# A part of one unit's attention moved beside the last MLP, and TensorE's order of the final two units written out

## The chip, the cores and the metric

The kernel runs on one core of a Trainium2 chip. The core has five engines with a queue each: TensorE (PE in the profile, its weight loads PEld), VectorE (DVE), ScalarE (ACT), GpSimd (POOL) and SyncE (SP), which here only issues DMA. The metric is the device time of one execution in microseconds. Three runs of the kernel before took 1056.87, 1057.65 and 1057.70 us; the median is 1057.65 us.

## The reference

Two transformer blocks are applied to x of shape (32, 64, 512), float32 throughout. Block 0 is attention with one key and value head and a gated MLP of width 2048; block 1 is attention alone, with a latent of width 128 for keys and values. Block 1, which the change is about, is:

```
mu  = mean(x); var = mean(square(x - mu))
h   = (x - mu) * rsqrt(var + eps) * (1 + scale[:, None]) + shift[:, None]
q   = h @ Wq.T                      # 16 heads of 32
c   = h @ Wkd.T                     # the latent, 128 wide
k   = c @ Wku.T ; v = c @ Wvu.T     # 4 heads of 32
q, k rotated by position
out = x + (softmax(q @ k.T / sqrt(32)) @ v) @ Wo.T
```

The sequence length is 64, so the mask of the reference hides nothing.

## The kernel before

**Tiling.** The 32 sequences are cut into eight units of four sequences (256 tokens). A unit lies in SBUF as four chunks of 128 features by 256 tokens. For each unit, `attention0` (block 0's attention and the norm before the MLP), the MLP and `attention1` (all of block 1) follow each other. The MLP is computed with seven products in place of eight for each two by two block (`first_products`, `last_products`, `down`), and the sums of a unit's down products fill four of the eight PSUM banks until its last step adds them to x (lines 969 to 983).

**Staging.** Pieces of different units are interleaved by generators. Each piece issues some matrix products and the work that follows them, then yields an estimated PE cost and a latency. `Order.run` takes the piece whose job has done the smallest share of its total, among those whose latency is over. While the MLP of unit u runs, `attention0` of unit u+1 and, through the job `chain`, `attention1` of units 0 to 5 run beside it (lines 1062 to 1076). `second(u)` yields at no cost until `down` has marked unit u as finished, and then runs `attention1(u)`.

**The tail.** When the MLP of unit 7 is through but for its last down step, that step and `second(6)` and `second(7)` are left (lines 1079 to 1114). They are jobs of rising rank: the down step first, then unit 6, then unit 7. Both units use a "lean" form of `attention1`. Its norm takes the mean as four accumulated products straight from x (eight matmul records, since one float32 product gives two records), squares by halves, sums the squares on PE by quarters (`root_by_quarters`), and spreads the root back over the partitions with four small products (`spread_out`). The form used beside the MLP instead adds the four chunks on POOL first and takes one product for each mean (`total_of`, `mean_of`), and its root is one operation over 256 columns.

**Order on the engines.** The program is handed to a scheduler that decides each engine's order from dependencies and its own estimate of time. Program order guides it but doesn't bind it. Only inside `with ordered(tc, PE)` (line 96) is PE's order that of the program; before the change this is used for the start of the kernel alone (`FIRST`, lines 1045 to 1047).

**Buffers.** Tiles of one tag share a fixed number of slots. In the tail `homes["now"]` lets small products take PSUM banks from all three tags (`at` 2, `gu` 2, `acc` 4) in turn. A dictionary for each of the two units (`sixth`, `seventh`) names the spare SBUF tiles that its values go to.

The steps that the prediction names are: `mean_of` (L466), the differences and squares (L758, L761), the scale on POOL (L763), `root_by_quarters` (L478, L470, L471), `spread_out` (L400), the second scale and shift (L771, L774), the projections (L525, named lat, q and po by their banks), keys and values (L804, L806), `rotate` (L533 to L536), the mask on the keys (L822), the copies of values (L828), the scores (L845), `softmax` (L545 to L555), `turned` (L560, L561), the contexts (L869, L878), and `output` (L573, L576).

Of the kernel before, what the change touches and what calls it, by code (L numbers as in the profile page):

```python
# [13 lines left out]
ALU = mybir.AluOpType  # L14
# [32 lines left out]
WARM = 11  # L47
STAY = 14103
FIRST = "aaaaaaa bb a mm aa bb a bbb aa b mm a bb aa a m b a b m b a b".replace(" ", "")
TWO_PI = float(np.nextafter(np.float32(2 * np.pi), np.float32(0)))  # L50


# [56 lines left out]
def two_blocks(ctx: ExitStack, tc: tile.TileContext, a: dict, out: bass.AP):  # L109
# [38 lines left out]
    make_identity(nc, ident)  # L148
    ones = fixed([P, P])
    nc.gpsimd.memset(ones, 1.0 / D)  # L150

    idle = bank("at", "idle")
    for _ in range(WARM):
        nc.tensor.matmul(idle[:, :P], ones, ones, start=True, stop=True)

    spread = fixed([P, US, P])
    nc.gpsimd.memset(spread, 0.0)
# [329 lines left out]
    def root_row(parts, eps, room, name):  # L487

        r = space(room, "r", UT, f"r_{name}")[:, :S]
        root_by_quarters(parts, eps, r, f"qs_{name}")  # L490
        pr = abank(f"row_{name}")[:, :UT]
        spread_out(pr.rearrange("p (b s) -> p b s", s=S), r)
        return pr
# [67 lines left out]
        nc.scalar.copy(pT, pp.rearrange("p c t -> p (c t)"))  # L561
        return pT

    def output(u, cT, w, name, last=False):

        x = x_units[u]
        for h in range(2):
            po = abank(f"po_{name}_{h}").rearrange("p (c t) -> p c t", c=2)
            for c in range(2):
                o = 2 * h + c  # L570
                project(po[:, c], w, slice(o * P, (o + 1) * P), cT)
            part = slice(2 * h, 2 * h + 2)
# [169 lines left out]
    def attention1(u, room):  # L742
        vb = room.get("vb", vblk1[u % 2])
        x = x_units[u]
        lean = "lean" in room
        h = tile4(room, "h", f"h1_{u}")
        if lean:
            mean = mean_of([x[:, k] for k in range(KC)], f"mean_{u}")
        else:
            sums = work("sq", [P, KC, UT], f"sum_{u}", 1)  # L750
            total = space(room, "tot", UT, f"tot_m{u}")
            nc.gpsimd.tensor_tensor(sums[:, 0:2], x[:, 0:2], x[:, 2:4], ALU.add)
            nc.gpsimd.tensor_tensor(total, sums[:, 0], sums[:, 1], ALU.add)
            yield 0.0, 6.0
            mean = mean_of([total], f"mean_{u}")
        sq = tile4(room, "h", f"sq1_{u}") if lean else work("sq", [P, KC, UT], f"sq1_{u}", 1)
        for part in (slice(0, 2), slice(2, 4)) if lean else (slice(0, 4),):
# [4 lines left out]
        parts = [sq[:, k] for k in range(KC)] if lean else [total_of(room, sq, f"v{u}")]  # L762
        nc.gpsimd.tensor_tensor(by_seq(h), by_seq(h), per_seq(s1, u), ALU.mult)  # L763
        yield 0.43, 3.0 if lean else 9.0
        if lean:
            r = root_row(parts, eps1, room, f"c{u}")
# [3 lines left out]
        for part in (slice(0, 2), slice(2, 4)) if lean else (slice(0, 4),):  # L770
# [3 lines left out]
            nc.gpsimd.tensor_tensor(by_seq(h[:, part]), by_seq(h[:, part]), per_seq(t1, u)[:, part], ALU.add)  # L774
        yield 0.43, 5.5 if lean else 9.0

        lat = abank(f"lat_{u}")
        project(lat[:, :UT], wkd, slice(0, LAT), h)
# [20 lines left out]

        query(0)  # L800
        yield 3.4, 0.0

        kv = abank(f"kv1_{u}")
        nc.tensor.matmul(kv[:, :UT], wkv1[:, 0], latT, start=True, stop=True)  # L804
        for t in range(2):
            nc.tensor.matmul(  # L806
                kv[:, UT + t * P : UT + (t + 1) * P], latT[:, t * P : (t + 1) * P], wkv1[:, 1], start=True, stop=True
            )
        kr = space(room, "kr", UT, f"kr_{u}").rearrange("p (b s) -> p b s", s=S)
        few = [P, US, S]  # L810
        rotate(
            kr,
            kv[:, :UT].rearrange("p (b s) -> p b s", s=S),
            cos.unsqueeze(1).to_broadcast(few),
            sin.unsqueeze(1).to_broadcast(few),
            few,
            f"k1_{u}",
        )
        kb = space(room, "kb", 2 * UT, f"kb1_{u}").rearrange("p (b g s) -> p b g s", b=US, g=2)
        wide = [P, US, 2, S]  # L820
        mask = kmask.unsqueeze(1).unsqueeze(3).to_broadcast(wide)
        nc.gpsimd.tensor_tensor(kb, kr.unsqueeze(2).to_broadcast(wide), mask, ALU.mult)  # L822
        for t in range(2):
            for b in range(2):
                v = kv[b * S : (b + 1) * S, UT + t * P : UT + (t + 1) * P]
                v = v.rearrange("p (m r d) -> p m r d", m=2, r=2)
                for r in range(2):
                    nc.scalar.copy(  # L828
                        vb[r * S : (r + 1) * S, 2 * t + b, :, r * HD1 : (r + 1) * HD1], v[:, :, r, :]
                    )  # L830
        yield 0.9, 0.0

        query(1)
        yield 3.4, 4.5

        cT = tile4(room, "h", f"cT1_{u}")
        def scores(t):
# [21 lines left out]
        def context(t, ps):  # L859
            pTs = []  # L860
            for m in range(2):
                name = f"1_{u}_{t}_{m}"
                pT = turned(ps[m], name, space(room, "pT", 512, f"pT{name}"))
                pTs.append(pT.rearrange("p (j t) -> p j t", j=4))
                yield 0.5, 1.2 * m
            cx = abank(f"cx1_{u}_{t}").rearrange("p (b c s) -> p b c s", b=2, c=KC)
            for b in range(2):
                for m in range(2):
# [10 lines left out]
            yield 1.0, 1.5 * t  # L879

        ps = []
        for t in range(2):
            ps.append(scores(t))

            yield 0.9, (0.0, 6.0)[t] if lean else 9.0
            if not lean:
                yield from context(t, ps[t])
# [170 lines left out]
    def behind():  # L1058
        for u in range(6):
            yield from second(u)  # L1060

    chain = Job(behind(), 0.8 * A1)
    for u in range(NU):
        now = Job(mlp(u), M)
# [15 lines left out]
    def spare(tag, cols, name, bufs=2):  # L1080
        return work(tag, [P, cols], f"own_{name}", bufs)

    zeros = spare("pT1", 512, "vb7", 2).rearrange("p (b r d) -> p b r d", b=US, r=2)
    nc.gpsimd.memset(zeros, 0.0)
    two = [spare("h2", 1024, f"h2{i}") for i in range(2)]
    few = spare("cs", 512, "few", 1)
    extra = spare("x", 1024, "kb6", XB)
    sixth = {
        "ring": "0",
        "lean": True,  # L1090
        "vb": vblk1[0],
        "p": [t[:, j * 512 : (j + 1) * 512] for t in two for j in range(2)],
        "latT": [few[:, :UT]],
        "kr": [few[:, UT:]],
        "kb": [extra[:, :512]],
        "pT": [extra[:, 512:], spare("pT0", 512, "pT6", 2)] * 2,
    }
    big = [spare("mw", 1792, f"mw{j}", MW) for j in range(4)]
    seventh = {
        "ring": "-",  # L1100
        "lean": True,
        "vb": zeros,
# [5 lines left out]
        "pT": [big[1][:, 1024:1536], big[2][:, 1024:1536]] * 2,  # L1108
# [86 lines left out]
```

## Time and profile before

| what | value |
|---|---|
| median of three runs | 1057.65 us |
| profiled execution, its own time | 1055.26 us |
| its span, first to last instruction | 1053.4 us |
| mean granted clock of TensorE | 0.989 |
| PE busy | 1012.6 us (96%) |
| PEld busy | 938.7 us (89%) |
| DVE / ACT / POOL busy | 546.7 / 329.1 / 432.8 us |
| MLP of unit 7, last product of its last down step | ends at about 980.4 us |
| last product of the kernel | ends at about 1049.6 us |

The span is the distance from the first to the last instruction of the profiled execution; its own time is 1.86 us longer, and 2.39 us shorter than the median of the runs. A timeline row is start, length, engine, line, operation and operands; successive rows of PE overlap a little, since matmuls are pipelined, so the work of a group is read from its start to the start of the next. In a table of stretches the columns are the length of the stretch, the busy time of each engine with its instructions, the granted clock (1.00 is full), the DMA share and GB/s.

### The profile page before, as it was taken

To read this page: it belongs to the slowest core of one execution; us is meant where nothing else is said; L and a number is where in the kernel's file an instruction comes from. 1 tells how busy PE (TensorE), PEld (TensorE's weight loads), DVE (VectorE), ACT (ScalarE), POOL (GpSimd) and SP (SyncE) were. 2 spreads that over 40 slices of the span, in tenths; PEclk is the share of its full clock that TensorE was granted. 3 is DMA by queue.
4 is the path that set the end of the run, shared out by engine and by line. 5 is a ranking of instruction groups with operands and counts; after the bars stand their busy time and mean duration, and the time that the engine had idled before them with its cause. 6 is when DMAs were issued, how large, how long until landed. Compare 5 with 4: busy or idle time off the path is not lost.

```text
span 1053.4 us, 21591 instructions
## 1 busy us (share of the span) xinstructions
PE 1012.6 (96%) x8602; PEld 938.7 (89%) x8602; DVE 546.7 (52%) x1377; ACT 329.1 (31%) x680; POOL 432.8 (41%) x518
## 2 busy tenths in 40 slices
PE   7899999999999999999999999999999999999887
PEld 6679999998999889989999989999999899999765
DVE  4966646545355385353555286532655345352363
ACT  4342112255114243142431332341424422141132
POOL 3424545443255443355341544234632335432541
PEclk8989999999999999999999999999999999999899
DMA  8816896463666364663555565465735547564001
GB/s 277 310 61 218 288 303 247 151 211 122 234 210 211 108 244 152 219 243 127 212 178 181 207 209 183 141 214 187 277 117 194 202 165 280 204 229 170 11 1 40
DMA packets 68275, 198.55 MB, mean 188 GB/s; under 512 B 7248, under 2 KB 15184, under 8 KB 67792
## 3 DMA queue, kind: packets, MB, share of 16 engines
q1 hardware_dynamic: 68176, 197.17, 53.4%
q8 instruction: 69, 1.13, 0.4%
q14 instruction: 30, 0.25, 0.1%
HBM read 180.37 MB, written 16.78 MB: 187 GB/s over the span
## 4 chain that ended last, share of the span: by engine, by line
PE 81%; DVE 8%; POOL 5%; DMA 2%; issue 2%; ACT 1%; SPq 0%; ACTq 0%; POOLq 0%; DVEq 0%
PE gu L899 34%; PE down L958 17%; PE po L525 10%; PE q L525 9%; DMA set<-in_wmlp 2%; PE cx L869 2%; PE sc L845 1%; PE lat L525 1%; PE pp L560 1%; PE sc L673 1%; PE kv L525 1%; PE cx L694 1%; DVE sm L553 1%; PE tab L400 1%; DVE mx L545 1%
## 5 line engine op out<-in xcount | busy, mean ns | idle before, releaser
L899 PE MATMUL gu<-h,set 128*128 128x128 f32 x2048 | 288.1, 277 | 6.4 <-DVE c L918 5.7
L899 PEld LDWEIGHTS gu<-h,set 128*128 128x128 f32 x2048 | 258.8, 192 | 15.5 <-issue 10.4
L899 PE MATMUL gu<-hc,set 128*128 128x128 f32 x1536 | 215.2, 275 | 0.0
L899 PEld LDWEIGHTS gu<-hc,set 128*128 128x128 f32 x1536 | 193.5, 192 | 1.0 <-issue 0.6
L937 POOL TENSOR_TENSOR act<-c,c 128x384 f32<-128x384 f32 x64 | 66.4, 1038 | 210.5 <-DVE c L925 140.8
L958 PE MATMUL down<-td,set 128*128 128x128 f32 x1024 | 137.5, 276 | 3.3 <-POOL td L940 2.5
L958 PEld LDWEIGHTS down<-td,set 128*128 128x128 f32 x1024 | 125.4, 192 | 5.2 <-POOL td L940 3.5
L911 ACT COPY e<-gu 128x128 f32<-128x128 f32 x128 | 33.7, 264 | 259.9 <-PE gu L899 246.8
L525 PE MATMUL q<-h,stays 128*128 128x256 f32 x480 | 111.3, 385 | 1.5 <-POOL h L774 1.5
L525 PE MATMUL po<-cT,stays 128*128 128x256 f32 x480 | 109.0, 382 | 2.1 <-DVE sm L553 2.1
L958 PE MATMUL down<-act,set 128*128 128x128 f32 x768 | 109.5, 278 | 0.0
L925 DVE TENSOR_TENSOR c<-gu,u 128x256 f32<-128x256 f32 x128 | 53.4, 419 | 106.4 <-PE gu L899 106.1
L525 PEld LDWEIGHTS q<-h,stays 128*128 128x128 f32 x480 | 90.9, 193 | 14.3 <-POOL h L774 1.7
L525 PEld LDWEIGHTS po<-cT,stays 128*128 128x128 f32 x480 | 89.8, 191 | 14.0 <-ACT cT L878 2.6
L958 PEld LDWEIGHTS down<-act,set 128*128 128x128 f32 x768 | 97.6, 192 | 5.2 <-issue 3.2
L913 DVE TENSOR_TENSOR u<-e,gu 128x128 f32<-128x128 f32 x128 | 35.9, 281 | 127.5 <-ACT e L911 126.8
L555 POOL TENSOR_TENSOR p<-p,sm 128x512 f32<-128x512 f32 x40 | 41.6, 1058 | 121.4 <-DVE sm L554 113.7
L536 POOL TENSOR_TENSOR qT<-u_q,v_q 128x512 f32<-128x512 f32 x30 | 38.1, 1269 | 97.2 <-DVE v_q L535 97.1
L573 DVE TENSOR_TENSOR x<-x,po 128x512 f32<-128x512 f32 x32 | 22.0, 687 | 87.7 <-PE po L525 87.7
L994 ACT ACT_TABLE_LOAD x34 | 43.6, 1283 | 54.5 <-DVE c L925 54.0
L939 POOL TENSOR_TENSOR td<-act 128x256 f32<-128x256 f32 x64 | 46.7, 730 | 5.6 <-DVE act L936 0.9
L994 ACT ACTIVATE c<-gu 128x128 f32<-128x128 f32 x64 | 17.7, 277 | 90.2 <-DVE c L925 82.2
(269 smaller groups left out, 1333.0 us busy)
## 6 DMA issues: line engine op xcount, KB each, us to landing
set<-sums SPq DMA_DIRECT2D x168, 512.0 KB, 5.6
set<-in_wmlp SPq DMA_DIRECT2D x192, 384.0 KB, 4.6
sums<-set SPq DMA_DIRECT2D x24, 512.0 KB, 4.1
x<-in_x SPq DMA_DIRECT2D x8, 512.0 KB, 5.5
out_x<-x SPq DMA_DIRECT2D x16, 256.0 KB, 2.3
mod<-in_mod SPq DMA_DIRECT2D x7, 512.0 KB, 5.2
a<-in_wmlp SPq DMA_DIRECT2D x24, 128.0 KB, 3.1
stays<-in_wo SPq DMA_DIRECT2D x2, 1024.0 KB, 8.0
```

The source lines that it names most:

```text
L525: nc.tensor.matmul(ps, w[:, k, cols], h[:, k, :], start=(k == 0), stop=(k == KC - 1))
L536: nc.gpsimd.tensor_tensor(dst, u, v, ALU.add)
L555: nc.gpsimd.tensor_tensor(p8, p8, sm.unsqueeze(2).to_broadcast(wide), ALU.mult)
L573: nc.vector.tensor_tensor(x[:, part], x[:, part], po, ALU.add)
L899: nc.tensor.matmul(ps, w[:, slot, k * P : (k + 1) * P], b[of][:, k], start=start and k == 0, stop=k == 1, skip_group_check=True)
L911: nc.scalar.copy(e, ps[:, 0])
L913: nc.vector.tensor_tensor(u2, e, ps[:, 1], ALU.add)
L925: nc.vector.tensor_tensor(c.rearrange("p (a b) t -> p a b t", b=2)[:, :, 1], ps[:, 2:4], u2.unsqueeze(1).to_broadcast([P, 2, HT]), ALU.add,)
L937: nc.gpsimd.tensor_tensor(act[:, 1:4], gate[:, 1:4], c[:, 1:4], ALU.mult)
L939: nc.gpsimd.tensor_tensor(td[:, 0:2], act[:, 1:3], act[:, 0:2], ALU.subtract)
L958: nc.tensor.matmul(sums_of[u][p][:, c], w[:, slot, c * P : (c + 1) * P], b[of], start=q % NP == 0 and i % 2 == 0 and c == 0, stop=q % NP = ...
L994: nc.scalar.activation(gate[2][:, 0], gate[0][:, 0], AF.Silu)
```

## The change

The change has four parts.

1. **Part of unit 6 moves beside the MLP of unit 7.** `second(6)` is made before the loop over the units, and while the MLP of unit 7 runs, `some` takes its first four pieces with a cost (`EARLY`): two of the norm, one of the latent, one of keys and values. In this part the norm has the form used beside the MLP (`slim` is false where a room is `early`), and keys and values come before the queries.
2. **The order of the tail on PE is written out.** After the loop, the last down step is issued, and then the string `LAST` gives the order of the remaining pieces: a for unit 6, b for unit 7, i for two products whose result nobody reads. The whole is inside `ordered`, so PE keeps it.
3. **Pieces are cut finer and reordered.** A lean query gives up its turn after each of its two chunks, the lean norm between the root and its spreading, and in the lean form all transposes of both halves (`turn`) come before the contexts. `output` in the lean form adds and stores each chunk by itself: four stores of 128 KB in place of two of 256 KB for a unit.
4. **Buffers.** The spare tiles of unit 6 are declared earlier, and both units have four separate places for transposed probabilities, where they had two used twice.

```diff
+EARLY = 4
+LAST = "aa b aa b iii b aa ii b bb bbb aa aa bb aa aaaa bbbb bb bbbb".replace(" ", "")
...
+    def idle(n):
+        idles["n"] += 1
+        ps = abank(f"idle_{idles['n']}")
+        for _ in range(n):
+            nc.tensor.matmul(ps[:, :P], ones, ones, start=True, stop=True)
...
         root_by_quarters(parts, eps, r, f"qs_{name}")
+        yield 0.5, 1.0
         pr = abank(f"row_{name}")[:, :UT]
...
+                if fine:
+                    nc.vector.tensor_tensor(x[:, o], x[:, o], po[:, c], ALU.add)
+                    nc.sync.dma_start(out[u][:, o], x[:, o])
+                    yield 1.7, 0.0
...
+        early = "early" in room
+        slim = lean and not early
...
-        if lean:
+        if slim:
             mean = mean_of([x[:, k] for k in range(KC)], f"mean_{u}")
...
+                if lean and c == 0:
+                    yield 1.7, 0.0
...
+        queries = [query(i) for i in range(2)]
+        if early:
+            kb = keys_values()
+            yield 0.9, 0.0
+        elif lean:
+            yield next(queries[0])
+            kb = keys_values()
+            yield 0.9, 0.0
+        for i, q in enumerate(queries):
+            yield from q
+            yield 1.7 if lean else 3.4, 4.5 * i
...
         if lean:
-            yield from context(0, ps[0])
-            yield from context(1, ps[1])
-        yield from output(u, cT, wo1, f"1_{u}", True)
+            pTs = []
+            for t in range(2):
+                pTs.append((yield from turn(t, ps[t])))
+            for t in range(2):
+                context(t, pTs[t])
+                yield 1.0, 1.5 * t
+        yield from output(u, cT, wo1, f"1_{u}", True, lean)
...
+    sixth = second(6, room6)
+    def some(pieces, n):
+        for cost, latency in pieces:
+            n -= cost > 0
+            yield cost, latency
+            if not n:
+                return
...
+        if u == NU - 1:
+            jobs.append(Job(some(sixth, EARLY), 5.0))
         chain.done -= chain.total if u > 1 else 0.0
         rest = order.run(jobs, until=tuple(must))
+    order.run([*rest, Job(down(NU * NP - 1), 3.0)])
     homes["now"] = everywhere
...
-    last = down(NU * NP - 1)
-    tail = [Job(second(6 + i, room), A1, 2 + i) for i, room in enumerate((sixth, seventh))]
-    order.run([*rest, Job(last, 3.0, 1), *tail])
+    ends = {"a": sixth, "b": second(7, room7)}
+    with ordered(tc, mybir.EngineType.PE):
+        for name in LAST:
+            if name == "i":
+                idle(2)
+            else:
+                next(ends[name])
+        for pieces in ends.values():
+            assert next(pieces, None) is None
```

More of the change, by code (lines that the diff above doesn't have):

```diff
@@ L150, in two_blocks @@
     nc.gpsimd.memset(ones, 1.0 / D)
-    idle = bank("at", "idle")
-    for _ in range(WARM):
-        nc.tensor.matmul(idle[:, :P], ones, ones, start=True, stop=True)
+    idles = {"n": 0}
+    def idle(n):
[3 more added lines that the diff above has]
+            nc.tensor.matmul(ps[:, :P], ones, ones, start=True, stop=True)
+    idle(WARM)
     spread = fixed([P, US, P])
@@ L562, in turned, with output @@
         return pT
-    def output(u, cT, w, name, last=False):
+    def output(u, cT, w, name, last=False, fine=False):
         x = x_units[u]
@@ L571, in output @@
                 project(po[:, c], w, slice(o * P, (o + 1) * P), cT)
+                if fine:
+                    nc.vector.tensor_tensor(x[:, o], x[:, o], po[:, c], ALU.add)
+                    nc.sync.dma_start(out[u][:, o], x[:, o])
+                    yield 1.7, 0.0
+            if fine:
+                continue
             part = slice(2 * h, 2 * h + 2)
@@ L755, in attention1 @@
             mean = mean_of([total], f"mean_{u}")
-        sq = tile4(room, "h", f"sq1_{u}") if lean else work("sq", [P, KC, UT], f"sq1_{u}", 1)
-        for part in (slice(0, 2), slice(2, 4)) if lean else (slice(0, 4),):
+        sq = tile4(room, "h", f"sq1_{u}") if slim else work("sq", [P, KC, UT], f"sq1_{u}", 1)
+        for part in (slice(0, 2), slice(2, 4)) if slim else (slice(0, 4),):
             nc.vector.tensor_tensor(
@@ L761, in attention1 @@
             nc.scalar.activation(sq[:, part], h[:, part], AF.Square)
-        parts = [sq[:, k] for k in range(KC)] if lean else [total_of(room, sq, f"v{u}")]
+        parts = [sq[:, k] for k in range(KC)] if slim else [total_of(room, sq, f"v{u}")]
         nc.gpsimd.tensor_tensor(by_seq(h), by_seq(h), per_seq(s1, u), ALU.mult)
-        yield 0.43, 3.0 if lean else 9.0
-        if lean:
-            r = root_row(parts, eps1, room, f"c{u}")
+        yield 0.43, 3.0 if slim else 9.0
+        if slim:
+            r = yield from root_row(parts, eps1, room, f"c{u}")
         else:
@@ L769, in attention1 @@
             inverse_root(mean_of(parts, f"var_{u}"), eps1, r)
-        for part in (slice(0, 2), slice(2, 4)) if lean else (slice(0, 4),):
+        for part in (slice(0, 2), slice(2, 4)) if slim else (slice(0, 4),):
             nc.vector.tensor_tensor(
@@ L774, in attention1 @@
             nc.gpsimd.tensor_tensor(by_seq(h[:, part]), by_seq(h[:, part]), per_seq(t1, u)[:, part], ALU.add)
-        yield 0.43, 5.5 if lean else 9.0
+        yield 0.43, 5.5 if slim else 9.0
         lat = abank(f"lat_{u}")
@@ L798, in query @@
             )
[L800 to L807, printed above, removed]
-            )
[L809 to L830, printed above, removed]
@@ L831, in attention1, with keys_values @@
-        yield 0.9, 0.0
-        query(1)
-        yield 3.4, 4.5
+        def keys_values():
+            kv = abank(f"kv1_{u}")
+            nc.tensor.matmul(kv[:, :UT], wkv1[:, 0], latT, start=True, stop=True)
+            for t in range(2):
+                nc.tensor.matmul(
+                    kv[:, UT + t * P : UT + (t + 1) * P], latT[:, t * P : (t + 1) * P], wkv1[:, 1], start=True, stop=True
+                )
+            kr = space(room, "kr", UT, f"kr_{u}").rearrange("p (b s) -> p b s", s=S)
+            few = [P, US, S]
+            rotate(
+                kr,
+                kv[:, :UT].rearrange("p (b s) -> p b s", s=S),
+                cos.unsqueeze(1).to_broadcast(few),
+                sin.unsqueeze(1).to_broadcast(few),
+                few,
+                f"k1_{u}",
+            )
+            kb = space(room, "kb", 2 * UT, f"kb1_{u}").rearrange("p (b g s) -> p b g s", b=US, g=2)
+            wide = [P, US, 2, S]
+            mask = kmask.unsqueeze(1).unsqueeze(3).to_broadcast(wide)
+            nc.gpsimd.tensor_tensor(kb, kr.unsqueeze(2).to_broadcast(wide), mask, ALU.mult)
+            for t in range(2):
+                for b in range(2):
+                    v = kv[b * S : (b + 1) * S, UT + t * P : UT + (t + 1) * P]
+                    v = v.rearrange("p (m r d) -> p m r d", m=2, r=2)
+                    for r in range(2):
+                        nc.scalar.copy(
+                            vb[r * S : (r + 1) * S, 2 * t + b, :, r * HD1 : (r + 1) * HD1], v[:, :, r, :]
+                        )
+            return kb
@@ L836, in attention1 @@
+        queries = [query(i) for i in range(2)]
[9 more added lines that the diff above has]
+            yield 1.7 if lean else 3.4, 4.5 * i
+            if not lean and i == 0:
+                kb = keys_values()
+                yield 0.9, 0.0
         cT = tile4(room, "h", f"cT1_{u}")
@@ L857, in scores, with turn @@
             return ps
-        def context(t, ps):
+        def turn(t, ps):
             pTs = []
@@ L865, in context @@
                 yield 0.5, 1.2 * m
+            return pTs
+        def context(t, pTs):
             cx = abank(f"cx1_{u}_{t}").rearrange("p (b c s) -> p b c s", b=2, c=KC)
@@ L878, in context @@
                 nc.scalar.copy(to[:, b], cx[:, b])
-            yield 1.0, 1.5 * t
         ps = []
@@ L886, in attention1 @@
             if not lean:
-                yield from context(t, ps[t])
+                pTs = yield from turn(t, ps[t])
+                context(t, pTs)
+                yield 1.0, 1.5 * t
         if lean:
-            yield from context(0, ps[0])
-            yield from context(1, ps[1])
-        yield from output(u, cT, wo1, f"1_{u}", True)
+            pTs = []
+            for t in range(2):
+                pTs.append((yield from turn(t, ps[t])))
+            for t in range(2):
+                context(t, pTs[t])
+                yield 1.0, 1.5 * t
+        yield from output(u, cT, wo1, f"1_{u}", True, lean)
     finished = set()
@@ L1060, in behind, with spare @@
             yield from second(u)
+    def spare(tag, cols, name, bufs=2):
+        return work(tag, [P, cols], f"own_{name}", bufs)
+    two = [spare("h2", 1024, f"h2{i}") for i in range(2)]
+    few = spare("cs", 512, "few", 1)
+    extra = spare("x", 1024, "kb6", XB)
+    room6 = {
+        "ring": "0",
+        "lean": True,
+        "early": True,
+        "vb": vblk1[0],
+        "p": [t[:, j * 512 : (j + 1) * 512] for t in two for j in range(2)],
+        "latT": [few[:, :UT]],
+        "kr": [few[:, UT:]],
+        "kb": [extra[:, :512]],
+        "pT": [extra[:, 512:]] + [spare("pT0", 512, f"pT6{i}", 2) for i in range(2)] + [spare("pT1", 512, "pT62", 2)],
+    }
+    sixth = second(6, room6)
[5 more added lines that the diff above has]
+                return
     chain = Job(behind(), 0.8 * A1)
@@ L1074, in two_blocks @@
             jobs.append(chain)
+        if u == NU - 1:
+            jobs.append(Job(some(sixth, EARLY), 5.0))
         chain.done -= chain.total if u > 1 else 0.0
         rest = order.run(jobs, until=tuple(must))
+    order.run([*rest, Job(down(NU * NP - 1), 3.0)])
     homes["now"] = everywhere
-    def spare(tag, cols, name, bufs=2):
-        return work(tag, [P, cols], f"own_{name}", bufs)
     zeros = spare("pT1", 512, "vb7", 2).rearrange("p (b r d) -> p b r d", b=US, r=2)
     nc.gpsimd.memset(zeros, 0.0)
[L1085 to L1097, printed above, removed]
     big = [spare("mw", 1792, f"mw{j}", MW) for j in range(4)]
-    seventh = {
+    room7 = {
         "ring": "-",
@@ L1107, in two_blocks @@
         "p": [spare(tag, 512, f"{tag}{i}") for tag in ("gate", "act") for i in range(2)],
-        "pT": [big[1][:, 1024:1536], big[2][:, 1024:1536]] * 2,
+        "pT": [big[1][:, 1024:1536], big[2][:, 1024:1536], big[3][:, 512:1024], big[3][:, 1024:1536]],
         "qT": [big[2][:, :1024]],
```

## The prediction

> **What bounds the kernel now.** I read the stretches first: the MLP of unit 7 against what comes after it.
>
> ```profile
> 864.00:980.40 116.40, 115.20 (x994) 111.19 (x993) 49.04 (x133) 30.46 (x70) 43.81 (x58) 1.00 0.60 211
> 980.40:1053.40 73.00, 58.90 (x446) 46.54 (x444) 34.98 (x73) 21.09 (x50) 27.08 (x26) 0.95 0.04 15
> ```
>
> Beside the MLP, PE is busy 115.20 of 116.40 us while DVE, ACT and POOL are busy 49, 30 and 44: a product added there costs its own length, and vector work is free as long as it is not in front of something PE awaits. In the tail PE stands still for 14 of 73 us, and the clock is not full. Next, the PE timeline of the tail shows where.
>
> ```profile
> 980.37 1.89 PE L466 MATMUL mean<-x,stays 128*128 128x256 f32 x8
> 982.93 1.99 PE L466 MATMUL mean<-x,stays 128*128 128x256 f32 x8 [0.67 <-POOL x L982]
> ...
> 986.91 1.08 PE L400 MATMUL row_c<-r_c,stays 128*128 128x64 f32 x8
> 987.92 0.65 PE L478 MATMUL qs_c<-own_mw,stays 128*32 128x64 f32 x30
> 990.09 2.07 PE L525 MATMUL q<-h,stays 128*128 128x256 f32 x4 [1.53 <-POOL h L774]
> 991.96 1.81 PE L400 MATMUL row_c<-own_mw,stays 128*128 128x64 f32 x8
> 993.56 3.48 PE L525 MATMUL lat<-h,stays 128*128 128x256 f32 x8
> ...
> 1003.79 1.89 PE L525 MATMUL lat<-own_mw,stays 128*128 128x256 f32 x8
> ...
> 1017.87 0.65 PE L560 MATMUL pp<-stays,own_h 128*128 128x128 f32 x4 [2.30 <-POOL own_h L555]
> ...
> 1028.70 7.17 PE L525 MATMUL po<-cT,stays 128*128 128x256 f32 x32 [2.10 <-DVE sm L553]
> ```
>
> The waits in this view sum to 10.0 us (0.67, 1.07, 1.53, 2.30, 0.35, 0.73, 2.10, 0.53, 0.74). The same latent takes 1.89 us at 1003.79 and 3.48 at 993.56: the clock. The stretches of it:
>
> ```profile
> 985.00:990.00 5.00, 2.46 (x72) 1.93 (x66) 3.50 (x6) 2.32 (x5) 4.11 (x4) 0.98 0.01 3
> 990.00:997.00 7.00, 6.91 (x21) 5.90 (x22) 1.28 (x2) 0.00 (x0) 3.09 (x4) 0.53 0.00 0
> 1015.00:1019.50 4.50, 1.85 (x12) 1.05 (x10) 3.97 (x11) 1.85 (x3) 2.42 (x3) 1.00 0.00 0
> ```
>
> After five microseconds of small products and waits in the norms, the clock is halved for about 6.8 us, which costs 3.4. From 980.4 the tail is thus about 55 us of products, 10 of waits, 3.4 of clock and 3.8 from the last product (1049.6) to the end.
>
> **Part 1, the early pieces.** Pitches come from the timeline: a chunk of projection (8 records of 256 columns) 1.73 us (1000.34 to 1003.79 for 16), keys and values 0.88 (999.46 to 1000.34). Added to the MLP stage: two means of 2 records each 0.43 + 0.43, latent 1.73, keys and values 0.88, together **3.5 us** of PE, all on the path. Taken from the tail: mean 1.73, sums of squares 0.65, row 1.01, latent 1.73, keys and values 0.88, together 6.0.
>
> The vector work that moves with them, by unit 5's rows in the same stage: POOL two sums (1.27 + 0.73) twice, scale 1.91, shift 1.91, keys 0.72 + 1.06, that is 9.6 us; DVE 1.22 + 1.75 (the root over 256 columns) + 1.21 + 1.3 for the keys; ACT 1.06, 0.47, 0.37, 1.74 and one or two table loads of 1.28. It goes into queues with half their time free, behind which stand the gate's products (L937 to L941) and so `down`. Cover gone, a 1.91 us POOL operation in front of them would hold PE that long. PE's waits for such things sum to some 12 us between 100 and 980 us, about 0.1 in 8 us. I reserve **0.5 us**; bounds are 0 and 9.6 (all of POOL's work uncovered). No DMA moves: these four pieces issue none. The time is ample: unit 6's x is done at about 889 and unit 5's latent came 33 us after its mean, so unit 6's keys fall near 925, with the MLP ending at 984.
>
> **Part 2, the tail's order.** I lay `LAST` out from the end of the last down step, PE in order. Other pitches: scores 1.90, a pair of transposes 0.88, contexts 1.08 for half a unit, sums of squares 0.65, row 1.01, an unread product 4 records for two at 0.112 (12 MLP records from 958.92 to 960.26). From a query's end to its rotated form is 3.42 us (1009.15 to 1012.57: DVE v, u, shuffle, POOL add).
>
> - q6 first half to 3.46; mean of 7 to 5.19. Its x is whole at 2.5 (982.88 before), so it doesn't wait; if it did, the second half of q6 would be queued behind it. q6 second half to 8.65.
> - Sums of squares of 7 to 9.30: its squares are ready by 7.2, behind q6's rotation on DVE. Three idle pieces (1.34) to 10.64. The root takes 1.3 us after the sums (988.57 to 989.85), so is ready near 10.6. Row to 11.65. Queued behind it are unit 6's scores, which wait until 8.65 + 3.42 = 12.07 anyway. The root and that rotation meet on DVE: **0.55** more, one reciprocal.
> - Scores of 6 to 15.87; two idle pieces (0.89) to 16.76. h of 7 is ready by 14.9 (DVE 1.28 and POOL 2.05, after the row), so these 0.89 cover nothing. Latent 18.49; q7 chunk 20.22; keys 21.10; other three chunks 26.29; four transposes of 6 to 28.05. The softmax of 6 had from 14 on; before, four of them took DVE and POOL about 10 us from the first score.
> - Scores of 7 need q7 rotated: 26.29 + 3.42 = 29.71, a **wait of 1.66** with unit 6's contexts and output queued behind it, which could have run. To 33.51. Contexts of 6 to 35.67, copies on ACT 0.72, output of 6 to 43.31. The softmax of 7 takes 10.2 us from 31.6 and is covered by that output.
> - Transposes of 7 to 45.07, contexts 47.23, copies 0.72, output to 54.87, last add 0.42. From the last add's end to the end was 3.06 (1050.34 to 1053.40). [...] I keep 3.06. With the 0.55, the end is at **58.9**.
>
> The tail goes from 73.0 to 58.9, that is 14.1 less: 3.4 clock, 6.0 - 2.2 products, about 6 of waits, 0.3 of the last add. Less 3.5 and 0.5 in the MLP stage, the sum is **-10.1 us**. The profiled execution took 1055.26 and would take 1045.2; its median stands 2.39 higher, so I forecast **1047.5**.
>
> **Part 3 and 4** cost nothing beyond this. The finer adds are 8 of 0.42 against 4 of 0.69 on DVE, of which only the last shows; SP issues 8 stores (0.33 each) against 4, and no load is behind them. The zeros for unit 7's values stay after the loop, 0.53 on POOL, well ahead of use.
>
> [...] From 26.3 to 29.7 PE runs only transposes and waits. The row of 1015.00 holds such a stretch: 2.30 idle, four transposes, 0.35 idle, four more, and the clock was 1.00 throughout. [...]
>
> **Rivals.**
>
> - **The clock falls once more in the tail**, as just said, or in the norm of 7 in spite of the idle products: 1050.9. [...] against it, the row at 1015 and full-size products on both sides.
> - **The MLP stage pays.** Unit 6's POOL and DVE work gets in front of the gate's: two or three of the 1.9 us operations uncovered give 4 us more, 1051.5, up to 9.6 - 0.5 more. Against it: stages before with a whole attention0 beside the MLP (150 to 250 us, DVE 50.6, POOL 45.0 of 100) had PE never idle.
> - **The order on DVE and POOL in the tail** is the scheduler's. If softmax and rotations are served in a poor order, behind a PE that can't step aside, some 5 us of the gain stay: 1052.5.
> - **Slower: unit 6's norm is late.** The scheduler could leave its early pieces to the end of the MLP stage. Then the first piece of `LAST` waits and everything on PE is behind it. From the first sum to h the durations above sum to about 14 us (2.0, 0.6, 1.2, 1.1, 2.0, 0.6, 1.8, 1.75, 1.2, 1.9), with the clock falling (3.4) it ends near 1065. It decides when h of 6 comes more than 10.1 us after the last down step. Against it: 60 us of slack.
>
> **How the numbers follow.** Forecast 0.62; clock 0.12; MLP stage 0.11 (0.08 faster, 0.02 the same, 0.01 slower); order on DVE 0.07 (0.06 and 0.01 the same); late norm 0.08. A change within 0.2% (2.1 us) is about what a measurement can't tell from none. Faster 0.88, same 0.03, slower 0.09. The forecast's own range is 1044.5 to 1050: without any of the waits and reserves (4.6 us: 0.42, 1.66, 0.72, 0.72, 0.55, 0.5) it would be 1042.9, and each could double. The low end of the whole range is that bound, 1042.9; the high end, 1053.5, takes in the clock, the DVE order and an MLP stage with 6 us of waits, and leaves out the late norm and the worst of the stage.
>
> **What would show it.** The latent and keys of 6 before 950 us; the last down step ending 3.5 to 4 later, near 984; full clock in the tail; a wait of one to two microseconds before unit 7's scores; 59 us from the last down step to the end. It is wrong if PE waits for h of 6, if `down` waits on POOL more than before, or if the clock drops again.

## The result, and the profile after

Four runs of the changed kernel took 1047.24 to 1051.62 us with a median of 1048.55, against 1057.64 before: 9.1 us less, a ratio of 0.9918 with a 95% interval of 0.9898 to 0.9937. The forecast was 1047.5 in a range of 1042.9 to 1053.5. The profiled execution took 1047.82 us, its span is 1046.0; before it was 1053.4, so in the profiles only 7.4 us are gained. Line numbers are those of the changed kernel from here on; in the kernels with a bank for each chunk they are one higher from the output on (L912 for L911).

The stretches of the changed kernel first: the MLP of unit 7, in nearly the same window as before, and the tail.

```profile
864.00:980.00 116.00, 115.94 (x987) 111.56 (x987) 53.83 (x138) 36.21 (x82) 50.31 (x61) 1.00 0.60 210
986.08:1046.00 59.92, 49.76 (x404) 40.71 (x402) 31.42 (x68) 17.43 (x38) 21.46 (x21) 1.00 0.06 18
```

Beside the MLP, DVE, ACT and POOL carry 5 to 6.5 us more each, and PE waits no more for them than before: from the mean product of unit 7's norm (ms_b below) to the end of the last down step its one wait in both profiles is 1.2 us for POOL (td, L940 before and L978 after). The tail is 59.9 us where it was 73.0, with 10 us of PE idle where there were 14, and the clock is full throughout. Then the PE timeline of the tail.

```profile
986.08 3.62 PE L535 MATMUL q<-h,stays 128*128 128x256 f32 x16
989.54 1.89 PE L475 MATMUL mean<-x,stays 128*128 128x256 f32 x8
...
997.43 1.08 PE L409 MATMUL row_c<-own_mw,stays 128*128 128x64 f32 x8 [0.44 <-DVE own_mw L480]
998.44 1.30 PE L875 MATMUL sc<-own_kb,qT 64*64 64x128 f32 x34
1000.05 1.10 PE L875 MATMUL sc<-own_kb,qT 64*64 64x128 f32 x30 [0.31 <-DVE own_mw L789]
1001.08 1.16 PE L161 MATMUL idle<-stays 128*128 128x128 f32 x8
1002.07 1.89 PE L535 MATMUL lat<-own_mw,stays 128*128 128x256 f32 x8
...
1015.19 1.54 PE L875 MATMUL sc<-own_mw,own_mw 64*64 64x128 f32 x48 [1.10 <-POOL own_mw L546]
...
1020.19 1.99 PE L535 MATMUL po<-cT,stays 128*128 128x256 f32 x8 [1.58 <-ACT cT L911]
1023.47 3.72 PE L535 MATMUL po<-cT,stays 128*128 128x256 f32 x16 [1.29 <-DVE x L583]
1027.71 1.99 PE L535 MATMUL po<-cT,stays 128*128 128x256 f32 x8 [0.51 <-DVE x L583]
...
1036.60 3.72 PE L535 MATMUL po<-own_mw,stays 128*128 128x256 f32 x16 [0.51 <-DVE x L583]
1040.84 1.99 PE L535 MATMUL po<-own_mw,stays 128*128 128x256 f32 x8 [0.51 <-DVE x L583]
```

PE starts on unit 6's queries at once, and the norm of unit 7 lies under them. What is new is in the outputs: the 32 records that ran without a break are now in pieces of 8, 16 and 8, and each break ends with an add on DVE (L583). In the list of waits of the changed kernel's tail (us in total, times, longest us) these breaks stand first.

```profile
PE po L535 <- DVE x L583: 2.8, 4, 1.3
PE po L535 <- ACT cT L911: 1.6, 1, 1.6
PE sc L875 <- POOL own_mw L546: 1.1, 1, 1.1
PE po L535 <- ACT own_mw L911: 0.7, 1, 0.7
PE row_c L409 <- DVE own_mw L480: 0.4, 1, 0.4
PE sc L875 <- DVE own_mw L789: 0.3, 1, 0.3
```

To set the kernels side by side I use three marks of each profile: the mean product of unit 7's norm before its MLP (ms_b), the first product after the last down step, and the end of the span.

| kernel | ms_b at | MLP stage | tail | median of its runs |
|---|---|---|---|---|
| before | 859.24 | 121.13 | 73.0 | 1057.64 |
| changed | 861.14 | 124.94 | 59.9 | 1048.55 |

The 7.4 us of the profiles are thus 13.1 in the tail, less 3.8 in the MLP stage, less 1.9 ahead of ms_b, where the change did nothing to the work. Over the profiles of the runs below this first mark lies anywhere from 858.40 to 863.09, and for the changed kernel itself at 861.14 and 862.77 in two profiles, so I take the 1.9 for chance. Without it the two stages give 9.3 us, close to the 9.1 of the medians.

### The profile page after: what moved, and what is told of

It reads as the page before. It is cut to its first block, busy times and chain, and to the rows that moved or that the text cites. A ratio compares the mean times of both kernels' runs of the same rounds, so it can differ in the third digit from the quotient of the medians.

```text
span 1046.0 us, 21558 instructions
## 1 busy us (share of the span) xinstructions
PE 1007.5 (96%) x8578; PEld 936.4 (90%) x8578; DVE 548.7 (52%) x1379; ACT 334.1 (32%) x683; POOL 436.4 (42%) x521
## 4 chain that ended last, share of the span: by engine, by line
PE 81%; DVE 8%; POOL 4%; DMA 4%; issue 2%; ACT 1%; SPq 0%; ACTq 0%; DVEq 0%; POOLq 0%
PE gu L937 33%; PE down L996 16%; PE q L535 10%; PE po L535 10%; DMA set<-in_wmlp 3%; PE sc L875 2%; PE pp L570 1%; PE cx L902 1%; PE lat L535 1%; PE sc L689 1%; PE kv L535 1%; PE cx L710 1%; DVE set L264 1%; DVE sm L563 1%; DMA x<-in_x 1%
## 5 line engine op out<-in xcount | busy, mean ns | idle before, releaser
L589 DVE TENSOR_TENSOR x<-x,po 128x512 f32<-128x512 f32 x28 | 19.2, 687 | 72.9 <-PE po L535 72.9
```

## The experiments

Two theories stood against each other after the result. The first: the sum of the prediction is right as it stands. The second: it came out near by two errors that cancel, since each unit's scores, charged 3.80 us, took 2 to 2.6, and the outputs, charged 6.92 us each, took 9.35 and 8.73.

The experiments were run in three series, each on another chip and each with the kernel before beside them; its medians were 1056.26, 1056.88 and 1055.56 us. Across series a ratio or the length of a tail is therefore a better measure than a median. A tail is that of one profile; for the changed kernel it was 59.9 and 60.0 in two.

**One add for two chunks.** The output of units 6 and 7 gets back its old form.

```diff
-        yield from output(u, cT, wo1, f"1_{u}", True, lean)
+        yield from output(u, cT, wo1, f"1_{u}", True)
-LAST = "aa b aa b iii b aa ii b bb bbb aa aa bb aa aaaa bbbb bb bbbb"
+LAST = "aa b aa b iii b aa ii b bb bbb aa aa bb aa aa bbbb bb bb"
```

> The output of units 6 and 7 goes back to one add and one store for two chunks; all else is as in the changed kernel. Theory, one bank for two chunks: PE waits for the add of a chunk before it writes the next chunk of the same PSUM bank (2.8 us of waits on L583 in four places, and about 0.26 us of pipeline for each), so the two outputs lasted 9.35 and 8.73 us where their products take 6.92 each. Without it they take 6.9 to 7.2 each, some 3.9 us come back, and the coarser last add and store take 0.6: about 3.3 us less than the changed kernel, near 1045.2. Theory of the prediction, the finer adds cost nothing but their last add: 0.3 to 0.6 us slower than the changed kernel, near 1049. From the last down step to the end: 56.6 us by the first, 60.4 by the second (59.9 in the changed kernel's profile).

Measured: 1044.09 us (1043.12 to 1046.19), ratio to before 0.9886 (0.9861 to 0.9910), a tail of 56.6 against 59.9. The finer output, as the changed kernel has it, costs 3.3 us.

**A bank for each chunk.** The finer adds stay, but no two chunks share a PSUM bank.

```diff
-            po = abank(f"po_{name}_{h}").rearrange("p (c t) -> p c t", c=2)
+            po = None if fine else abank(f"po_{name}_{h}").rearrange("p (c t) -> p c t", c=2)
             for c in range(2):
                 o = 2 * h + c
-                project(po[:, c], w, slice(o * P, (o + 1) * P), cT)
+                pc = abank(f"po_{name}_{o}")[:, :UT] if fine else po[:, c]
+                project(pc, w, slice(o * P, (o + 1) * P), cT)
                 if fine:
-                    nc.vector.tensor_tensor(x[:, o], x[:, o], po[:, c], ALU.add)
+                    nc.vector.tensor_tensor(x[:, o], x[:, o], pc, ALU.add)
```

> The finer adds and stores stay, but each chunk of the output has a PSUM bank to itself. Theory, one bank for two chunks: the four waits on L583 go, 3.9 us less than the changed kernel, near 1044.6, and from the last down step to the end about 56.0 us. Rival, the waits are for the add itself or for DVE's queue, whatever the bank: no change, 59.9 us.

Measured: 1043.97 us (1042.42 to 1044.60), ratio 0.9877 (0.9850 to 0.9904), a tail of 56.0, as expected by the first of its theories. PE's timeline of this kernel has both outputs whole again.

```profile
1020.88 7.17 PE L535 MATMUL po<-cT,stays 128*128 128x256 f32 x32 [1.58 <-ACT cT L912]
...
1032.44 7.17 PE L535 MATMUL po<-own_mw,stays 128*128 128x256 f32 x32 [0.74 <-ACT own_mw L912]
```

So it is what two chunks shared and not the add. In the changed kernel PE begins the second chunk of a bank only when the add that reads the first one has ended: the four adds end at 1023.42, 1027.65, 1036.55 and 1040.78, and PE goes on 0.05 to 0.06 us later. The edit gives each chunk a tile of its own as well as a bank, so whether the dependency was drawn for the bank or for the tile isn't shown. The wait is paid four times: three times 0.51 us, and 1.29 where DVE was still in a softmax. Each time some 0.26 us more is lost at the break, which is an estimate: a row of 8 records lasts 1.99 us after a wait, against 1.73 from start to start in an unbroken row.

**No unread products.**

```diff
-LAST = "aa b aa b iii b aa ii b bb bbb aa aa bb aa aaaa bbbb bb bbbb"
+LAST = "aa b aa b b aa b bb bbb aa aa bb aa aaaa bbbb bb bbbb"
```

> All five pieces of unread products are left out; the order is otherwise the same. Theory of the clock: without them PE has the sums of squares, a wait of about 1.8 us and the row in the norm of unit 7, the clock halves for 6.8 us as before the change, and the kernel is 3.4 - 0.9 = 2.5 us slower than the changed one, near 1051. Rival, PE is busy enough on either side: the clock stays at 1.00 in the tail, the first three pieces only covered a wait, and the last two (0.99 us from 1001.08 to 1002.07) were in the way: 0.9 us faster, near 1047.7.

Measured: 1047.50 us (1046.29 to 1050.40), ratio 0.9919 (0.9892 to 0.9947), a tail of 60.0: no difference. Neither theory foresaw it so. The row started 11.35 us after the last down step as in the changed kernel, since PE waited 1.96 us for the root in place of 1.60 of unread products and 0.44 of waiting. Then the clock did fall in this profile, but for some 3.4 us in place of 6.8 (estimated from the 0.58 below; from 998 to 1001 it was 0.50), and what that cost is what the second place of unread products had cost: from the first score of unit 6 to the end of unit 7's latent both kernels take 5.36 us. The wait and the stretches, without unread products:

```profile
996.15 1.08 PE L409 MATMUL row_c<-own_mw,stays 128*128 128x64 f32 x8 [1.96 <-DVE own_mw L480]
```

```profile
994.00:997.00 3.00, 1.04 (x23) 0.91 (x12) 2.00 (x5) 1.60 (x2) 1.49 (x2) 1.00 0.00 0
997.00:1001.00 4.00, 4.00 (x69) 3.51 (x68) 3.53 (x6) 0.33 (x1) 2.05 (x2) 0.58 0.00 0
```

**The early pieces alone.** The tail is handed back to the job list, and with it to the scheduler's own order. The finer pieces stay; the unread products, which stand in `LAST`, go with it.

```diff
-    ends = {"a": sixth, "b": second(7, room7)}
-    with ordered(tc, mybir.EngineType.PE):
-        for name in LAST:
...
+    tail = [Job(pieces, A1, 2 + i) for i, pieces in enumerate((sixth, second(7, room7)))]
+    order.run(tail)
```

> The early pieces of unit 6 and the finer pieces stay, but the tail is handed to the job list by rank as before the change, with the scheduler's own order on PE and no unread products. If moving the early pieces is most of the gain: near 1049 to 1051. If the written order is most of it: within 2 us of the kernel before, 1056 to 1058. My own sum: early pieces take 6.0 of products and unit 6's norm from the tail and give 3.5 to the MLP, but unit 7's norm has then nothing ahead of it in rank except unit 6's queries, and waits of 4 to 6 us stay; near 1051.5.

Measured: 1061.16 us (1059.23 to 1063.92, 9 runs), ratio to before 1.0050 (1.0035 to 1.0065): slower than before, which none of the three expectations held. The MLP stage is 124.95 us, as with the order; the tail is 74.2. Two of its stretches and two lines of its PE timeline:

```profile
1005.00:1012.00 7.00, 5.49 (x16) 4.19 (x17) 4.21 (x11) 2.22 (x4) 5.20 (x6) 0.53 0.00 0
1036.00:1049.00 13.00, 7.40 (x28) 4.40 (x30) 6.51 (x14) 4.67 (x8) 4.13 (x4) 0.50 0.00 0
```

```profile
1033.86 1.10 PE L875 MATMUL sc<-own_mw,own_mw 64*64 64x128 f32 x32 [2.40 <-POOL own_mw L546]
...
1040.19 2.11 PE L570 MATMUL pp<-stays,own_gate 128*128 128x128 f32 x8 [5.23 <-POOL own_gate L565]
```

The scheduler spends unit 6's output before unit 7's scores. When those are there, nothing is left to lie beside unit 7's softmax; PE waits 5.23 us, and the clock is at 0.50 for 13 us. With the earlier stretch (0.53) that is about 20 us near half clock, in which PE's busy 12.9 us would, by estimate, have been about half as long: the 8 transposes at 1040.19 last 2.11 us, and 8 at full clock in the changed kernel 1.04 (at 1029.54). The lack of unread products cost nothing under the written order; what they would have done in this one isn't tested.

**The order alone.** Unit 6 has nothing beside the MLP, the lean norm as before, and PE's order for both units is written out.

```diff
-        "early": True,
...
-        if u == NU - 1:
-            jobs.append(Job(some(sixth, EARLY), 5.0))
-LAST = "aa b aa b iii b aa ii b bb bbb aa aa bb aa aaaa bbbb bb bbbb"
+LAST = "a b iii a iii a b iii b aaaaaa bbb aa bbb aa aa bb aa aaaa bbbb bb bbbb"
```

> Nothing of unit 6 runs beside the MLP: its whole block 1, in the lean form of the norm, is in the tail, and the order on PE is written out for both units, with nine pieces of unread products in three places of the norms. Theory, the written order is what pays and the early pieces add to it: the tail gets 6.0 us of products more than in the changed kernel and about 3 more of waits in the norms and scores, the MLP stage gets 3.8 back; 5 to 6 us slower than the changed kernel and some 3 faster than before, near 1053.5. Rival, neither part pays alone: within 2 us of the kernel before or slower, as the early pieces alone were. MLP stage from unit 7's last norm to its last down step: 121.1 us as before (124.9 with the early pieces).

Measured: 1057.04 us (1056.49 to 1058.47, 12 runs), ratio 1.0009 (0.9999 to 1.0018): no gain, as the rival had it. The MLP stage is 121.14, the tail 72.6. This tail also has the bank waits of the finer output (2.4 us), waits of 2.5 before unit 6's transposes, and a fall of the clock after them (0.50 from 1024 to 1026, 0.66 from 1026 to 1028), so it is taken up once more below.

**Contexts first.** Unit 6's contexts go ahead of unit 7's scores.

```diff
-LAST = "aa b aa b iii b aa ii b bb bbb aa aa bb aa aaaa bbbb bb bbbb"
+LAST = "aa b aa b iii b aa ii b bb bbb aa aa aa bb aaaa bbbb bb bbbb"
```

> One exchange in the written order: unit 6's two contexts come before unit 7's two scores. Theory, the wait for unit 7's rotated queries (1.1 us) and the wait of unit 6's output for its copied contexts (1.58) are each other's cover: unit 6's output starts 2.9 us sooner, and the kernel ends 2.5 to 2.9 us sooner, near 1045.5. Rival, the softmax of unit 7, which isn't moved, takes over: its last row on POOL ends about 40 us after the last down step, and unit 7's last transposes wait for it, so 1 us or less is gained.

Measured: 1048.64 us (1048.26 to 1050.17), a tail of 60.7, against 1048.92 of the changed kernel in the same series: nothing gained in time. The output did start 2.9 us sooner (31.2 us after the last down step in place of 34.1), and the gain was gone at its first break:

```profile
1017.59 1.99 PE L535 MATMUL po<-cT,stays 128*128 128x256 f32 x8
1022.88 5.41 PE L535 MATMUL po<-cT,stays 128*128 128x256 f32 x16 [3.29 <-DVE x L583]
```

```profile
1022.41 0.41 DVE L583 TENSOR_TENSOR x<-x,po 128x256 f32<-128x256 f32 x1
```

The add that PE waits for (the row of DVE above) stands in DVE's queue behind half of unit 7's softmax, from 1016.84 to 1022.41. Starting sooner only lengthened the wait to 3.29 us, and the clock fell after it (0.57 from 1023 to 1027). The rival had named unit 7's softmax, but expected it to hold up unit 7's last transposes and not the output of unit 6.

**The changed kernel again**, in the same series.

> The changed kernel itself, once more, beside the others on one chip: 1048.5 with a spread of about 4 us between executions, as the first four had (1047.2 to 1051.6). Theory: the spread comes from the first 100 us, where the clock is still changing, and from the middle, not from the tail: 124.9 us for the MLP of unit 7 and 59.9 for the tail again.

Measured: 1048.92 us (1046.15 to 1050.87), ratio to before 0.9928 (0.9908 to 0.9948); ms_b at 862.77, the MLP stage 124.96, the tail 60.0. The last two are the same to 0.1 us in a run whose span is 1.7 us longer than that of the first profile: the difference (1.6 us) is all ahead of ms_b. Of the expected theory only that much is shown, that the spread doesn't come from the tail. The clock does change in the first 100 us: in the first profile it was 0.83 to 20 us, 1.00 from there to 50, 0.90 to 100, and 1.00 from 100 to 980.

**Both mends.** A bank for each chunk, contexts first, and the second place of unread products left out.

```diff
-LAST = "aa b aa b iii b aa ii b bb bbb aa aa bb aa aaaa bbbb bb bbbb"
+LAST = "aa b aa b iii b aa b bb bbb aa aa aa bb aaaa bbbb bb bbbb"
(and the lines of the bank for each chunk)
```

> A PSUM bank for each chunk of the output, contexts of unit 6 before the scores of unit 7, and the second place of unread products (two pieces) left out; the first three stay. Sum: 3.9 + 2.9 + 0.9 less than the changed kernel, less some 0.5 that the softmax of unit 7 takes back: 52.5 us from the last down step to the end, 7.2 us faster than the changed kernel, near 1041. If the clock falls without the second place of unread products, up to 1.7 us less is gained.

Measured: 1039.98 us (1038.28 to 1042.96), a ratio to before of 0.9849 (0.9826 to 0.9873), a tail of 53.15. This beats both kernels: 8.9 us faster than the changed one in its series. What is left of waits in its tail, by the list of waits:

```profile
PE pp L570 <- POOL own_act L565: 1.2, 1, 1.2
PE po L535 <- ACT own_mw L912: 0.7, 1, 0.7
PE row_c L409 <- DVE own_mw L480: 0.4, 1, 0.4
```

With a bank for each chunk, the exchange that was worth nothing by itself pays: unit 6's output now starts 29.8 us after the last down step and takes 7.0. The tail is 6.8 us shorter than the changed kernel's. The banks alone gave 3.9 of it, and by the marks 1.3 are gained up to the end of unit 7's latent, where the unread products left; so the exchange is worth some 1.5. That is an estimate by difference, since no run has the exchange with the banks alone.

**The order alone, mended.** As the order alone, with the banks and the contexts first.

```diff
-LAST = "a b iii a iii a b iii b aaaaaa bbb aa bbb aa aa bb aa aaaa bbbb bb bbbb"
+LAST = "a b iii a iii a b iii b aaaaaa bbb aa bbb aa aa aa bb aaaa bbbb bb bbbb"
(against the order alone; and the lines of the bank for each chunk)
```

> The order alone once more (nothing of unit 6 beside the MLP), now with a PSUM bank for each chunk of the output and unit 6's contexts before unit 7's scores. Against the kernel with both mends and the early pieces (1039.98, 53.2 us of tail, 124.95 of MLP) this is what the early pieces are worth in a tail that isn't held up by the banks. Theory: they take 6.0 us of products and 5 to 6 of waits in the norm of unit 6 and its softmax from the tail and give 3.8 to the MLP, so this kernel is 7 to 8 us slower than that one, near 1047.5, and about 9 faster than before. Rival: the tail is bound by the chain of norms and softmaxes of unit 6, which the order can't fill, and most of the gap to the kernel before stays closed: 1053 or more.

Measured: 1052.01 us (1050.21 to 1055.56, 9 runs), ratio to before 0.9970 (0.9952 to 0.9988), a tail of 67.5, an MLP stage of 121.13. This lies between the two expectations and nearer to the rival. The order alone is worth 3.5 us by the medians of its series, or 5.5 by its tail, once the banks don't hold it up; the early pieces on top of it are worth about 12 by the medians (from different series) or 10.5 by the stages (14.3 in the tail, less 3.8). Waits before unit 6's transposes (2.1 us) and a fall of the clock (0.50 from 1022 to 1024, 0.71 from 1024 to 1026) are still in it: with unit 6's norm in the tail, its scores come 14.5 us later (26.9 us after the last down step in place of 12.4), and its softmax has too little beside it.

**Both mends, no unread products.**

```diff
-LAST = "aa b aa b iii b aa b bb bbb aa aa aa bb aaaa bbbb bb bbbb"
+LAST = "aa b aa b b aa b bb bbb aa aa aa bb aaaa bbbb bb bbbb"
(against both mends; the lines of the bank for each chunk stay)
```

> As the kernel with both mends, without any unread products. With the first three pieces away, PE waits about 2 us for the root, and in the run without unread products the clock then fell to half for 3.8 us. If that comes again: 1.3 to 1.9 us slower than the kernel with both mends, near 1041.6, tail 54.8. If the clock stays at 1.00: equal to it, near 1040, tail 53.2, since the pieces only stood where PE waits.

Measured: 1040.95 us (1040.11 to 1042.58), ratio to before 0.9863 (0.9844 to 0.9883) against 0.9849, a tail of 53.1: equal within what the runs can tell. The wait and the stretches of the norm, as shown above for the first kernel without unread products:

```profile
996.55 1.08 PE L409 MATMUL row_c<-own_mw,stays 128*128 128x64 f32 x8 [1.96 <-DVE own_mw L480]
```

```profile
994.00:997.00 3.00, 1.04 (x37) 0.90 (x37) 2.36 (x5) 1.60 (x2) 1.56 (x2) 1.00 0.00 0
997.00:1001.00 4.00, 3.93 (x76) 3.27 (x76) 3.27 (x6) 0.15 (x1) 2.37 (x3) 1.00 0.00 0
```

PE is busy 1.04 of 3 us in both; in the one profile the clock then fell to 0.58 and in the other it stayed at 1.00.

## Why the prediction was right

The direction, the size and the place were right: the tail gives, the MLP stage takes. That the number came so near is in part luck, and twice over. In the sum two errors nearly cancel, as the steps below show. And the profiled execution, which was to take 1045.2 us, took 1047.82: 1.0 more in the tail and 1.9 ahead of ms_b, less 0.2 in the MLP stage. The median stands 0.7 above it and not 2.39 as before, and so came back to the forecast. By the prediction's own steps, from the marks:

| step | predicted | measured |
|---|---|---|
| MLP stage | +3.5 and 0.5 in reserve | +3.8 |
| queries of 6, mean and sums of 7 | 9.30 | 9.31 |
| idle products, row | 2.9 | 3.05 |
| scores of 6, idle products, waits | 5.1 | 3.6 |
| latent to last query of 7 | 9.5 | 9.5 |
| transposes of 6, wait, scores of 7 | 7.2 | 5.1 |
| contexts of 6, copies | 2.9 | 3.5 |
| output of 6 | 6.9 | 9.35 |
| transposes, contexts, copies of 7 | 4.6 | 4.6 |
| output of 7 | 6.9 | 8.7 |
| last add to the end | 3.5 | 3.2 |
| tail | 58.9 | 59.9 |

- **The early pieces** were right. Their latent came at 918.09 and their keys and values at 932.66 (rows below), where 925 was forecast for the keys and 950 was the bound; the stage grew by 3.8 us in every kernel that has them (124.94 to 124.96). The rival of an MLP stage that pays, and that of a late norm, are out.

```profile
918.09 1.89 PE L535 MATMUL lat<-h,stays 128*128 128x256 f32 x8
...
932.66 0.60 PE L822 MATMUL kv<-own_few,stays 128*128 128x256 f32 x2
```

- **The scores** were mis-sized. The row of 64 records at 1.90 us is both halves of a unit; the prediction charged it for each half, 3.80 for a unit. In the changed kernel they took 2.64 us for unit 6, a wait of 0.31 included, and about 2.1 for unit 7 without its wait, which is some 3 us less than charged.
- **"Part 3 and 4 cost nothing beyond this"** is the step that failed. It looked for the price of the finer output on DVE and SP, where none shows, and put the wait of PE between two chunks of a bank at nothing without a reason. The two outputs took 4.2 us more than their products, of which the runs show 3.9 (1043.97 with a bank for each chunk and a tail of 56.0 against 59.9) to come from sharing a bank or its tile. With the scores' error of the other sign the two nearly cancel, and the tail was 59.9 where 58.9 was forecast.
- **The copies before unit 6's output** were given 0.72 us from a row where ACT had nothing else. Here ACT was in unit 7's exponentials (1.17 us from 1017.89), and PE waited 1.58.
- **The clock** stayed at 1.00 through the tail of the changed kernel, as the row had it. But it was less of a test than the prediction held, since PE ran more there than transposes: between them and the wait (from 1011.59 to 1015.19, PE busy 2.50 of 3.60 us) 16 records of unit 7's scores ran. That such a stretch could bring a second drop was the author's estimate, and the runs show both: 1.00 around the row at 1015 in the kernel before, and 0.50 from 1024 to 1026 in the order alone, after unit 6's transposes with 2.5 us of waits at them and 1.3 more at unit 7's scores. That the idle products are what held the clock isn't shown either: without them it fell to 0.58 in one profile, stayed at 1.00 in another, and the time was the same in both pairs of kernels (1047.50 and 1040.95 us, ratios of 0.9919 and 0.9863, against 0.9918 and 0.9849 with them).
- **The order on DVE and POOL** cost little in the changed kernel and not the 5 us of its rival. But it is real: the add behind a softmax held PE for 1.29 us where the others held it for 0.51, and with contexts first for 3.29, which took back the whole gain.
- **What the parts are worth** the prediction didn't ask. As they stand in the changed kernel, neither gives anything alone: early pieces without the order 1061.16, the order without them 1057.04. With the banks and the contexts mended, the order alone gives 3.5 us by the medians. The early pieces take work away from PE in the tail, and in the scheduler's own order too little was left to lie under the softmax of unit 7: PE waited 5.23 us, and the clock was 0.50 from 1036 to 1049.

## What to carry to other kernels

Before the add that empties a PSUM bank is split so that the first half can leave sooner, look at whether both halves share the bank or its tile. In these kernels the writer then waited for the reader between them, for 0.51 us (by estimate 0.26 more was lost each time), and for 3.29 where the reader's queue was long. When work is moved out of a latency-bound end, what it leaves must still be laid under the chains that stay, and an order by rank may not do that; write the order down and check which long chain has which products beside it. And when a sum comes out right, compare it step by step: two errors of about three and four microseconds stood in this one.

## What the runs showed of the hardware

The same instructions did and did not bring a fall of the clock. Two kernels with the same products and the same 1.96 us wait in the norm of unit 7 had it once at 0.58 for 4 us and once not at all (1.00), in one profile each. In the kernel with contexts first it fell after a wait of 3.29 us (0.57 from 1023 to 1027), and in the kernel before it was 1.00 from 1015.00 to 1019.50, around a wait of 2.30 us. What decides between a fall and none isn't shown. With the early pieces alone the clock fell before the long wait of 5.23 us was over: when 1.1 us of it had passed, after 6 us in which PE was busy for 2.56 (before 1036.00 it was 1.00, from 1036.00 to 1038.00 it was 0.52). It stood at half (0.50) up to 1049 through the wait and the broken work after it.

The kernel before took 1052.84 to 1060.53 us over the series, a wider spread than its first runs showed, so a difference of a few microseconds between two profiles has to be read from marks inside them.
